# Issue order in an attention block: urgent exponentials and bank-emptying instructions, a later broadcast of 1/l, and outer sums laid elsewhere

## The chip, the cores and the metric

One core of one Trainium2 chip. Times are device microseconds of one execution; medians are given with the number of runs, and kernels are compared by the ratio of their mean times in the same rounds on the same chip (said again with the result). All quoted runs were in the fast state; the 41 runs of the kernel before that stand beside e1 lie within 0.31% (3239.23 to 3249.20 us). That matters here, because most differences are around 1%.

## The reference, cut to what matters

A block over 16 images of 512 channels and 32 x 32 pixels, all in float32:

```python
xn = group_norm(x, 8 groups)                       # per image
q, k, v = split(qkv_w @ xn + qkv_b)                # 512 -> 3 x 512
attn = softmax(q^T k / sqrt(128)) per head         # 4 heads, 1024 x 1024
out = x + proj_w @ (v attn^T) + proj_b
```

## The kernel before: the parts that the argument touches

The four heads of an image run one after the other. A head has 8 steps; in a step TensorE makes the transposed scores of 128 keys against 1024 queries in two halves, ScalarE takes their exponentials, and one step later TensorE adds v times those exponentials into a PSUM tile (PSUM is the memory that takes TensorE's results in this kernel; one 128 x 512 tile of it is called a bank here). TensorE's spare room in a head is filled with the big matrix products of a neighbouring image: q and k in heads 0 and 2, the projection in head 1, v in head 3. They are done by two levels of Strassen-like products, so VectorE makes sums of input blocks ("outer sums" t1 to t4 of the image, "inner sums" of their halves) and PSUM banks are emptied often, by copies on ScalarE and adds on VectorE.

The code is traced in program order and a scheduler then orders each engine's queue, by priority (which is the trace order, unless told otherwise) and by its own estimate of when things are ready. What stands ahead in a queue can cost time on the chip: in the trace of the kernel before, ScalarE was idle for 7.92 us before a copy that stood behind a transfer's issue (at 169.68 us, shown in the prediction).

The emptying of banks, which the change touches (cut):

```python
def kept_copy(n):                                   # in strassen(): x is a PSUM bank
    t[n] = upool.tile([P, HALF], F32, tag=n, ...)
    nc.scalar.copy(t[n][:, :width], t["x"][:, :width])

def out_(which, a, c=None):                         # in two_levels(): a is a PSUM bank
    ...
    if c is None:
        nc.scalar.copy(dst, view(a))
    else:
        nc.vector.tensor_add(dst, view(a), view(c))
```

The products of a group go by turns into a bank x and a bank y and mostly add to what is there already, so the product after next cannot start before the emptying is done (in the trace of the kernel before, v_y is held up so 30 times, for 13.7 us in sum and 0.7 at most). The broadcast of 1/l, the inverse of the softmax denominators, goes through DRAM: 1024 numbers are written as a row and read back onto all 128 partitions. Both transfers are issued on ScalarE's queue:

```python
def spread_inverse(b, h, step):
    if step == 0:
        row = rows_of[b, h] = dpool.tile([1, N], F32, ...)          # in DRAM
        nc.scalar.dma_start(row.rearrange(...), inverse.pop((b, h)))  # row <- r
        return
    rinv[b, h] = lpool.tile([P, N], F32, ...)
    nc.scalar.dma_start(rinv[b, h], rows_of.pop((b, h)).to_broadcast((P, N)))

for half in range(NH2):                             # in the loop over steps
    scores(s, half)                                 # matmul and exponential
    if j == 1 and s > NB:
        spread_inverse(*where(s - NB)[:2], half)
```

The second issue has to wait until the row has landed, which took 1.3 to 6.4 us from the row's issue in the trace of the kernel before (median 2.3, 63 rows). The image is normalised on ScalarE in steps 5 and 6 of head 1 of the image before, and its outer sums follow in steps 6 and 7.

## Time and profile before

| | before |
|---|---|
| median of the 3 runs at hand before the prediction | 3247.06 us (3245.63 to 3248.78) |
| span of the profiled execution | 3251.7 us |
| late starts of TensorE in it, in sum | 110.4 us |
| of these, before the first score | 12.4 us |
| tail | 2.3 us |

"Late starts" is the measure that the whole document uses. The records of two matmuls that follow each other without a hitch begin 0.429 us apart after a 512-wide one and 0.216 us after a 256-wide one (medians in the trace of the kernel before). Counted from a slightly lower line, 0.427 and 0.213 us, which the author set just below the smallest such intervals of that trace (0.428 and 0.215), whatever an interval has above it is a gap, and all gaps over 50 ns are summed. The page's own idle times are smaller, because a matmul's end is modelled and lies up to 0.17 us into the gap (a 512-wide record lasts 0.594 us in the mean, the next begins after 0.429). The lines of the page and of the waits are shown in the prediction below. In all such lines PE is TensorE, PEld its weight loads, DVE VectorE, ACT ScalarE, POOL GpSimd and SP SyncE; a q (ACTq) marks the issue of a transfer. A line in order of time has its start, its length (us), engine, source line, operation and `output<-inputs`; in brackets stands the idle time before it and what ended that.

### The profile page before, as it was taken

What the parts mean: (1) busy time and instruction counts of PE and PEld (TensorE: products, weight loads), DVE (VectorE), ACT (ScalarE), POOL (GpSimd) and SP (SyncE); (2) the same over time, 40 slices, a digit from 0 to 9 for tenths busy, and PEclk for the clock granted to TensorE, in tenths of its full rate; (3) what the DMA queues carried; (4) which work ended last, traced back from release to release, by engine and by line L of the source; (5) the groups of instructions that cost most, each with busy time, mean ns of one, the idle gap of its engine ahead of it and who ended that gap; (6) DMA issues with size and microseconds to landing.
All of it is one profiled execution on the core that took longest, in us unless ns stands there. A gap on an engine that the chain in (4) does not pass through costs nothing.

```text
span 3251.7 us, 34056 instructions
## 1 busy us (share of the span) xinstructions
PE 3185.4 (98%) x10474; PEld 2178.0 (67%) x10474; DVE 2633.3 (81%) x4625; ACT 1439.8 (44%) x2709; POOL 516.3 (16%) x922
## 2 busy tenths in 40 slices
PE   8999999999999999999999999999999999999999
PEld 6566666766666766667666666666666666666664
DVE  8868878788787888878788787987879878788784
ACT  2534435354353543535435354353534535344442
POOL 0011121111211112111121111212012120121100
PEclk9999999999999999999999999999999999999999
DMA  5555553545545455454554545545455453555531
GB/s 161 186 192 164 180 172 123 186 153 182 172 142 181 145 194 161 161 161 146 187 162 162 169 132 193 164 165 167 136 180 171 164 173 134 182 160 172 181 124 40
DMA packets 209388, 526.92 MB, mean 162 GB/s; under 512 B 32816, under 2 KB 65840, under 8 KB 209200
## 3 DMA queue, kind: packets, MB, share of 16 engines
q1 hardware_dynamic: 128992, 276.88, 27.5%
q0 software_dynamic: 66240, 212.39, 19.5%
q10 hardware_dynamic: 13968, 35.41, 3.4%
q8 instruction: 86, 1.41, 0.2%
q14 instruction: 102, 0.84, 0.1%
HBM read 389.56 MB, written 135.00 MB: 161 GB/s over the span
## 4 chain that ended last, share of the span: by engine, by line
PE 47%; issue 27%; DVE 16%; DMA 7%; POOL 2%; ACT 1%; ACTq 0%; POOLq 0%; SPq 0%; DVEq 0%
PE po L867 13%; PE s L772 13%; PE qk_x L548 6%; PE qk_y L548 5%; PE pp_x L548 4%; DVE qk_t L518 3%; PE pp_y L548 3%; DMA vd<-vu 2%; DVE xt L277 2%; DMA out_y<-y 2%; DMA y<-in_x 2%; DMA v<-vd 1%; DVE qk_r L567 1%; DVE vu L703 1%; DVE tot L785 1%
## 5 line engine op out<-in xcount | busy, mean ns | idle before, releaser
L772 PE MATMUL s<-qk,qk 128*128 128x512 f32 x2048 | 1049.0, 594 | 4.5 <-ACT p L777 4.3
L867 PE MATMUL po<-p,v 128*128 128x512 f32 x2048 | 1053.2, 596 | 0.0
L777 ACT ACTIVATE p<-s 128x512 f32<-128x512 f32 x1024 | 610.0, 596 | 895.9 <-PE s L772 817.1
L867 PEld LDWEIGHTS po<-p,v 128*128 128x128 f32 x2048 | 602.0, 303 | 319.1 <-issue 202.3
L785 DVE TENSOR_TENSOR tot<-tot,p 128x1024 f32<-128x1024 f32 x385 | 470.4, 1222 | 147.9 <-ACT p L777 146.2
L772 PEld LDWEIGHTS s<-qk,qk 128*128 128x128 f32 x2048 | 387.0, 190 | 114.1 <-issue 43.5
L548 PE MATMUL qk_x<-qk_t,w 128*128 128x256 f32 x1344 | 356.8, 384 | 9.4 <-DVE qk_t L518 3.5
L548 PEld LDWEIGHTS qk_x<-qk_t,w 128*128 128x128 f32 x1344 | 250.2, 190 | 170.0 <-issue 66.2
L448 ACT COPY qk_u<-qk_x 128x512 f32<-128x512 f32 (+1 forms) x256 | 136.1, 532 | 262.2 <-PE qk_x L548 208.3
L711 POOL DMA_DIRECT2D vd<-vu x120 | 66.3, 552 | 992.4 <-DVE vu L703 990.7
L567 DVE TENSOR_TENSOR qk_r<-qk_y,qk_u 128x512 f32<-128x512 f32 (+1 forms) x256 | 158.3, 619 | 40.1 <-ACT qk_u L448 26.3
L548 PE MATMUL pp_x<-pp_t,w_proj 128*128 128x256 f32 x630 | 170.8, 388 | 6.7 <-ACT pp_p L448 6.7
L567 DVE TENSOR_TENSOR v_r<-v_y,v_u 128x512 f32<-128x512 f32 (+1 forms) x120 | 76.5, 638 | 112.2 <-ACT v_u L448 82.0
L548 PE MATMUL v_x<-v_t,w_v 128*128 128x256 f32 x630 | 166.7, 381 | 0.0
L522 POOL DMA_DIRECT2D kept_t<-qk_t x240 | 129.2, 540 | 233.4 <-DVE qk_t L518 188.7
L756 POOL DMA_DIRECT2D out_y<-y x120 | 66.2, 552 | 627.4 <-DVE y L755 595.2
L548 PEld LDWEIGHTS pp_x<-pp_t,w_proj 128*128 128x128 f32 x630 | 114.0, 190 | 76.4 <-issue 22.5
L548 PEld LDWEIGHTS v_x<-v_t,w_v 128*128 128x128 f32 x630 | 118.6, 190 | 55.2 <-issue 19.1
L716 POOL DMA_DIRECT2D v<-vd x240 | 140.0, 590 | 83.8 <-issue 60.0
L548 PE MATMUL qk_y<-x,w 128*128 128x256 f32 x512 | 143.5, 382 | 0.0
L448 ACT COPY v_u<-v_x 128x512 f32<-128x512 f32 (+1 forms) x124 | 66.2, 534 | 164.8 <-PE v_x L548 125.0
L646 DVE SCALAR_TENSOR_TENSOR qk<-qk_r,qkb_sb,qk_r 128x512 f32<-128x512 f32 x192 | 137.3, 743 | 1.6
(204 smaller groups left out, 4486.0 us busy)
## 6 DMA issues: line engine op xcount, KB each, us to landing
w<-kept SPq DMA_DIRECT2D x90, 512.0 KB, 4.1
kept_t<-qk_t POOLq DMA_DIRECT2D x180, 256.0 KB, 4.4
v_t<-kept_t SPq DMA_DIRECT2D x180, 256.0 KB, 3.0
w<-kept SPq DMA_DIRECT2D x90, 384.0 KB, 3.9
rinv<-row ACTq DMA_DIRECT2D x63, 512.0 KB, 5.4
x<-in_x POOLq DMA_DIRECT2D x60, 512.0 KB, 5.0
vd<-vu POOLq DMA_DIRECT2D x120, 256.0 KB, 3.4
v<-vd POOLq DMA_DIRECT2D x240, 128.0 KB, 4.6
```

The lines of the kernel that those rows point to most:

```text
L448: nc.scalar.copy(t[n][:, :width], t["x"][:, :width])
L518: nc.vector.tensor_sub(to[:, i, :], inner_block(g, i, a), inner_block(g, i, c))
L522: nc.gpsimd.dma_start(t, to)
L548: nc.tensor.matmul(acc[:, ts(i, Q)], have["w"][t][:, i, slot, :], inner(i, bn), start=(first and i == 0), stop=True, skip_group_check=True,)
L567: nc.vector.tensor_add(dst, view(a), view(c))
L646: nc.vector.scalar_tensor_tensor(st[b, h][:, ts(half, HALF)], a, qkb_sb[:, i : i + 1], c, ALU.add, ALU.add)
L711: nc.gpsimd.dma_start(rows[which][ts(h, P), :], u)
L716: nc.gpsimd.dma_start(vs[b, pair][ts(q, BLK), half].rearrange("m h (k i) j -> m (h k) (i j)", k=n), rows[which].rearrange("(k m) (q e) -> ...
L772: nc.tensor.matmul(sc, ks[b, h][:, ts(j, P)], qs[b, h][:, ts(half, HALF)], start=True, stop=True)
L777: nc.scalar.activation(ps[s][:, ts(half, HALF)], sc, AF.Exp, scale=SCALE)
L785: added[b, h, j] = nc.vector.tensor_add(tot[b, h][:, i], tot[b, h][:, i], ps[s][:, i])
L867: nc.tensor.matmul(po[b, h][:, i], v_block(b, h, j), ps[s][:, i], start=(j == 0), stop=(j == NB - 1),)
```

## The change

Its intent: what TensorE waits for directly (exponentials, and copies and adds that empty PSUM banks) is put ahead of other work in the scheduler's choice; the broadcast is issued a step later, when its row has mostly landed; the image's outer sums are traced close to the step that reads them. No instruction is added or removed. `high_priority(40)` ranks an instruction as if it had been traced 40 instructions earlier. `issue_after(i)` keeps instructions behind `i` in its engine's queue; this part is called the pin below.

```diff
+URGENT = 40
...
-            nc.scalar.copy(t[n][:, :width], t["x"][:, :width])
+            with tc.high_priority(URGENT):
+                nc.scalar.copy(t[n][:, :width], t["x"][:, :width])
...
-                if c is None:
-                    nc.scalar.copy(dst, view(a))
-                else:
-                    nc.vector.tensor_add(dst, view(a), view(c))
+                with tc.high_priority(URGENT):
+                    if c is None:
+                        nc.scalar.copy(dst, view(a))
+                    else:
+                        nc.vector.tensor_add(dst, view(a), view(c))
...
-        nc.scalar.activation(ps[s][:, ts(half, HALF)], sc, AF.Exp, scale=SCALE)
+        with tc.high_priority(URGENT):
+            exps[s] = nc.scalar.activation(ps[s][:, ts(half, HALF)], sc, AF.Exp, scale=SCALE)
...
-                    plan[6 + r].append(lambda r=r: x_sums(b + 1, (r + 1,)))
+                plan[6].append(lambda: x_sums(b + 1, (1,)))
...
         elif h == 2:
             spread(plan, staggered(qk_groups(b + 1, 0)), 0, NB)
+
+            plan[0].insert(2, lambda: x_sums(b + 1, (2,)))
+            plan[1].append(lambda: x_sums(b + 1, (3,)))
...
-                if j == 1 and s > NB:
-                    spread_inverse(*where(s - NB)[:2], half)
+                if j in (1, 2) and half == 1 and s > NB:
+                    with tc.issue_after(exps[s].ins):
+                        spread_inverse(*where(s - NB)[:2], j - 1)
```

(Row 1 of the outer sums is t1, row 2 is now t2 alone, and the new row 3 is t3 and t4. Callers of the sums of o are adapted so that they do the same as before.)

More of the change, by code (lines that the diff above doesn't have):

```diff
@@ L271, in halves, with sums_of_b @@
         return b
-    def sums_of_b(b, rows=(1, 2), chunks=range(KC)):
+    def sums_of_b(b, rows=(1, 2, 3), chunks=range(KC)):
         def sub(o, i, j):
@@ L282, in sums_of_b, with x_sums @@
             sub("t2", "b22", "t1")
+        if 3 in rows:
             sub("t3", "t2", "b11")
             sub("t4", "b21", "t2")
-    def x_sums(b, rows=(1, 2)):
+    def x_sums(b, rows=(1, 2, 3)):
         if 1 in rows:
@@ L761, in fast_path @@
     ps, tot, po, rinv, last_eviction = {}, {}, {}, {}, {}
-    inverse, rows_of, added = {}, {}, {}
+    inverse, rows_of, added, exps = {}, {}, {}, {}
     steps = B * HEADS * NB
@@ L971, in last_projection @@
         l, recip = last_division(b, HEADS - 1)
-        sums_of_b(bl, (2,), (1,))
+        sums_of_b(bl, (2, 3), (1,))
         for r in range(2):
@@ L1046, in plan_head @@
                 plan[3].append(lambda: sums_of_b(ob[b], (1,)))
-                plan[5].append(lambda: sums_of_b(ob[b], (2,), (0,)))
+                plan[5].append(lambda: sums_of_b(ob[b], (2, 3), (0,)))
         elif h == 2:
             spread(plan, staggered(qk_groups(b + 1, 0)), 0, NB)
+            plan[0].insert(2, lambda: x_sums(b + 1, (2,)))
+            plan[1].append(lambda: x_sums(b + 1, (3,)))
         else:
```

## The prediction

> **What bounds the kernel now.** I read the page's busy shares first, then the order of time on TensorE, then the waits, and last the order of time around the longest gaps.
>
> ```profile
> PE 3185.4 (98%) x10474; PEld 2178.0 (67%) x10474; DVE 2633.3 (81%) x4625; ACT 1439.8 (44%) x2709; POOL 516.3 (16%) x922
> ```
>
> TensorE's matmul row is busy for 98% of the span of 3251.7 us; nothing else is near. But the ends of matmul records are modelled, so I measure TensorE by starts. TensorE in order of time, in a stretch where nothing holds it up:
>
> ```profile
> 999.87 1.02 PE L772 MATMUL s<-qk,qk 128*128 128x512 f32 x2
> 1000.73 1.02 PE L867 MATMUL po<-p,v 128*128 128x512 f32 x2
> 1001.59 0.60 PE L548 MATMUL qk_x<-qk_t,w 128*128 128x256 f32 x2
> 1002.02 1.02 PE L772 MATMUL s<-qk,qk 128*128 128x512 f32 x2
> ```
>
> A pair of 512-wide records takes 0.86 us from start to start (1000.73 - 999.87), so 0.43 each; a 256-wide one 0.215 (0.43 / 2). The trace holds 4155 of the first kind (2048 scores, 2048 weighted sums, some of the last projection) and 6188 of the second: 4155 x 0.428 + 6188 x 0.2155 = 1778 + 1334 = about 3112 us. The change removes no matmul, so this stays. The rest of the span, 3252 - 3112 = 140 us, is all there is to win. About 110 us of it are intervals between matmul starts that are over 50 ns too long: counted in the trace, 511 of them, 12.4 us before the first score at 69.8 us, 95.6 us in the main part, 2.3 us in the tail. The other 30 us are TensorE's idle beginning (its first matmul starts at 10.6 us) and the end (stores, the test of the flag), which the change doesn't touch.
>
> Who ends those gaps, from the view of waits (time in total, times, longest):
>
> ```profile
> ACT qk_p L448 <- DMA row<-r: 54.6, 12, 7.9
> PE v_y L548 <- DVE v_r L567: 13.7, 30, 0.7
> PE qk_y L548 <- DVE qk_t L518: 8.5, 14, 1.3
> PE pp_x L548 <- ACT pp_p L448: 6.7, 14, 1.5
> PE s L772 <- ACT p L777: 4.3, 6, 2.3
> PE qk_x L548 <- ACT qk_p L448: 3.5, 1, 3.5
> ```
>
> The reader is to see counts of 14 and 30: the same few places in each of the images (14 with an image before and after them; twice in 15). The lengths here are too small, since a modelled matmul end covers up to 0.17 us of each gap; by starts, the v_y gaps are 0.62 us in the mean, not 0.46.
>
> One such place for each cause, in order of time. VectorE, head 3 of image 5, a gap before v_y:
>
> ```profile
> 1239.63 1.25 DVE L877 TENSOR_TENSOR o<-o,rinv 128x1024 f32<-128x1024 f32 x1
> 1240.76 0.72 DVE L567 TENSOR_TENSOR v_r<-v_y,v_u 128x512 f32<-128x512 f32 x1
> 1241.54 1.13 PE L548 MATMUL v_y<-xt,w_v 128*128 128x256 f32 x4 [0.35 <-DVE v_r L567]
> ```
>
> The bank is emptied by v_r, whose other input was ready at 1238.7 (a copy begun at 1238.11 that takes 0.58), yet the division of 1.25 us was queued first. ScalarE, head 1 of the same image: a batch of normalisations stands before an exponential and a copy:
>
> ```profile
> 1143.92 2.93 ACT L82 ACTIVATE x<-x,sh,sc 128x512 f32<-128x512 f32 x4 [1.64 <-DVE sh L75]
> 1146.76 0.57 ACT L777 ACTIVATE p<-s 128x512 f32<-128x512 f32 x1
> 1147.24 0.35 ACT L448 COPY pp_p<-pp_x 128x256 f32<-128x256 f32 x1
> 1147.64 0.70 PE L548 MATMUL pp_x<-pp_t,w_proj 128*128 128x256 f32 x2 [0.38 <-ACT pp_p L448]
> ```
>
> And ScalarE's queue in image 0, with the broadcast of 1/l:
>
> ```profile
> 162.83 0.32 ACTq L816 DMA_DIRECT2D row<-r  x1
> 169.32 0.33 ACTq L821 DMA_DIRECT2D rinv<-row  x1
> 169.68 0.58 ACT L448 COPY qk_p<-qk_x 128x512 f32<-128x512 f32 x1 [7.92 <-DMA row<-r]
> 170.16 1.09 ACT L777 ACTIVATE p<-s 128x512 f32<-128x512 f32 x2
> ```
>
> From 162.8 to 169.3 the queue waits for the row to land before it can issue the load that reads it, and a copy and two exponentials stand behind.
>
> [...]98% busy, yet 110 us of late starts. [...]the copy behind the blocked issue lost 7.92 us. So order in the queue, which the change edits, decides. [...]The trace has 0.69 us for x's outer sums and 1.22 for tot: every non-urgent VectorE instruction costs an urgent one up to 1.2 us[...]. [...]Here row<-r lands after 1.3 to 6.4 us, median 2.3.
>
> **The change part by part.** No instruction is added or removed; all is order. Gaps below are sums over all images, by starts[...].
>
> 1. Urgent emptying of banks (copies and the adds or copies into R). The two v_y places in head 3 hold 12.6 + 9.3 = 21.9 us over 15 images. Taking the add at the next free slot saves a division of 1.13 us at one and a transpose of 1.1 at the other; both exceed the gap. I count 80%: -18 us. The pp_x place behind normalisations, 10.6 us over 14 images (0.65 plus 0.11 for the second matmul): one normalisation of 0.8 at most now stands before the copy, which was ready over 1 us earlier: -10.5.
> 2. Urgent exponentials. Image 0's gap of 2.4 us at 151.2 (2.92 us of normalisations before the exponential) goes: -2.4. In image 15 a bias that waits 3.5 us for a load stands before copies (1.8 us of gaps): -1.
> 3. The broadcast one step later (a step is about 6.2 us: 49.5 us of a head / 8), after that step's exponential. The row has landed by then in the median. The 54.6 us of ScalarE's idle time were mostly slack; what reached TensorE is 5.2 us at head 0's scores (11 to 13 images) and 5.3 in image 0: -4 and -4.
> 4. Outer sums of the image. Six subtractions of 0.69 (0.6 pipelined) stood ahead of head 2's inner sums. The four of t3 and t4 now come a step later, which takes 4 x 0.6 = 2.4 us out of the front. The gaps there (qk_y 13.3, qk_x 6.2, together 19.5 us over 14 images, 1.4 each) are shorter than 2.4. But t2 now falls behind the denominators (1.24 + 1.21 + about 1.3 of small ones = 3.7 us), and group 1's first product needs t2; it came late already in three images (3.7 us). I count half of 19.5: -10.
> 5. Small gaps of about 0.1 us (a weight load released late): some 25 us in all, mostly left: -2.
>
> Sum: -18 - 10.5 - 2.4 - 1 - 4 - 4 - 10 - 2 = -52 us. Against it, what is pushed back: inner sums qk_t and pp_t are not urgent yet TensorE needs them, and each urgent add can delay them by 0.7 us. I allow 1 us an image, 16 us. Net -36: 3247 - 36 = 3211 us.
>
> **The rivals.** (a) The wait only moves. VectorE is 81% busy, and in heads 1 to 2 it runs without a pause from 1143.8 to 1155.4; what urgent adds gain, inner sums, t2 and normalisation lose. For it: t2 behind the denominators could cost up to 2.5 us an image, 35 us, about all of the gain: 3240 to 3250. Against it: the v_y places are followed by work with slack. (b) Nearly every gap goes, as ScalarE is only 44% busy: 75 us less, 3172. Against: the 0.1 us gaps and the weight loads behind semaphores, and the start, have other causes. (c) The scheduler orders by its own estimates, so a new order can put a blocked DMA in front of ScalarE elsewhere; two us an image would make it 3240.
>
> **Range and chances.** 2% is 65 us, 59% of all late starts, and more than my gross sum: faster 0.05. Slower by 2% would need 4 us of new gaps in every image: 0.01. Within 2%: 0.94. Range 3188 to 3240.
>
> **What would show it.** Step 1: the v_y <- v_r and pp_x <- pp_p waits shrink from 13.7 and 6.7 us to under 4 together. Step 3: ScalarE's idle on row<-r falls from 54.6 to under 15. Step 4: the qk_y <- qk_t wait halves; if qk_x <- xt grows over 10 us, rival (a) has it. Busy times of all engines stay within 1%. I am wrong if late starts stay near 110 us in sum, or fall under 45.

## The result, and the profile after

| | before | after |
|---|---|---|
| median time, 4 runs each | 3247.92 us (3245.63 to 3251.33) | 3214.26 us (3210.56 to 3216.90) |
| ratio of the fast runs | | 0.9895, 95% interval 0.9878 to 0.9912 |
| span of the profiled execution | 3251.7 us | 3208.4 us |
| late starts in it | 110.4 us | 67.5 us |

A ratio here is the mean time of one kernel's fast runs over that of the other's fast runs of the same rounds, so it isn't quite the ratio of the medians. The difference of the medians is 33.7 us; the predicted one was 36. The profiled execution of before is a slow one of its kind and that of after the fastest, so their difference, 43.3 us, is larger.

TensorE does the same work, and its record shrinks only by gaps. The engines' line of the page of the changed kernel:

```profile
PE 3166.4 (99%) x10474; PEld 2181.6 (68%) x10474; DVE 2630.8 (82%) x4625; ACT 1442.0 (45%) x2709; POOL 528.8 (16%) x922
```

Late starts account for the whole difference: 3251.7 - 110.4 = 3141.3 us before, 3208.4 - 67.5 = 3140.9 after. This remainder is between 3140 and 3142 us in every profile of this study, whatever the kernel. So each experiment below can be read from its gaps alone.

Where they went, by place (sums over all images):

| place | before, us | after, us |
|---|---|---|
| head 3: v_y behind an add into v_r | 21.9 | 1.6 |
| start of head 2: products of the next image's q and k | 28.8 | 14.0 |
| end of head 1: pp_x behind a copy | 13.4 | 9.5 |
| start of head 1: pp_x | 0 | 4.7 |
| head 0, step 2: scores behind an exponential | 5.2 | 0 |
| image 0, head 2 | 8.1 | 5.7 |
| image 15, head 0 | 2.0 | 1.0 |
| before the first score | 12.4 | 10.2 |
| all the rest (many of about 0.1 us) | 18.6 | 20.8 |

The view of waits of the changed kernel (time in all, times, longest):

```profile
PE qk_y L553 <- DVE qk_t L523: 6.2, 6, 2.0
PE pp_x L553 <- ACT pp_u L453: 5.7, 14, 0.4
...
ACT v_r L571 <- DMA row<-r: 4.7, 4, 1.2
...
PE qk_x L553 <- DMA w<-kept: 2.8, 1, 2.8
...
ACT qk_r L571 <- DMA row<-r: 2.4, 2, 1.2
```

The 30 waits of v_y for v_r are no longer in the list, ScalarE's idle time behind the row fell from 57.2 us (54.6 of it before qk_p) to 4.7 + 2.4, and two waits of TensorE are there that were not before: pp_x now waits for pp_u where it waited for pp_p, and qk_x once for a load of weights. In order of time, the first place of the prediction (image 5, head 3) now reads

```profile
1224.96 0.72 DVE L573 TENSOR_TENSOR v_r<-v_y,v_u 128x512 f32<-128x512 f32 x1
1225.57 1.25 DVE L884 TENSOR_TENSOR o<-o,rinv 128x1024 f32<-128x1024 f32 x1
1225.93 1.03 PE L553 MATMUL v_y<-xt,w_v 128*128 128x256 f32 x4
```

The add stands ahead of the division, and v_y starts 0.87 us after the weighted sum before it, with no gap. At the end of head 1 the gap has moved by one product instead:

```profile
1137.32 0.81 ACT L85 ACTIVATE x<-x,sh,sc 128x512 f32<-128x512 f32 x1
1138.02 0.36 ACT L453 COPY pp_u<-pp_x 128x256 f32<-128x256 f32 x1
1138.44 0.70 PE L553 MATMUL pp_x<-pp_t,w_proj 128*128 128x256 f32 x2 [0.40 <-ACT pp_u L453]
```

The product before it began at 1136.58 and was through at about 1137.2; a normalisation took ScalarE at 1137.32, and the urgent copy came after its 0.8 us. Urgent here means next in the queue as the scheduler saw it, not an interruption.

In image 0 the wait for the row gave its place to another, a load of weights:

```profile
162.28 0.33 ACTq L828 DMA_DIRECT2D rinv<-row  x1
...
166.15 1.74 PE L553 MATMUL qk_x<-x,w 128*128 128x256 f32 x4 [2.83 <-DMA w<-kept]
```

And the gap costs more than its own length. Two stretches around it (length; busy time and number of instructions of PE, PEld, DVE, ACT and POOL; granted TensorE clock; share of the DMA engines; GB/s):

```profile
163.00:166.00 3.00, 0.32 (x1) 0.00 (x0) 3.00 (x5) 1.09 (x2) 0.53 (x1) 1.00 0.95 316
166.00:170.00 4.00, 3.85 (x10) 3.14 (x11) 0.54 (x2) 0.59 (x1) 0.00 (x0) 0.57 1.01 373
```

TensorE stood still in nearly all of the first stretch, and in the next its granted clock is 0.57 (0.5 from 166.47 to 169.88 us in the clock record): seven 256-wide products after the gap start 0.43 us apart in place of 0.22. The kernel before had the same after its gap of 3.7 us there (clock 0.5 from 170.81 to 174.22 us). This will matter in the experiments.

### The profile page after: what moved, and what is told of

The parts are those of the page before. It is cut to its first block, busy times and chain, and to the rows that moved or that the text cites. A ratio compares the mean times of both kernels' runs of the same rounds, so it can differ in the third digit from the quotient of the medians.

```text
span 3208.4 us, 34028 instructions
## 1 busy us (share of the span) xinstructions
PE 3166.4 (99%) x10474; PEld 2181.6 (68%) x10474; DVE 2630.8 (82%) x4625; ACT 1442.0 (45%) x2709; POOL 528.8 (16%) x922
## 4 chain that ended last, share of the span: by engine, by line
PE 72%; DVE 19%; issue 4%; DMA 4%; POOL 1%; ACT 0%; SPq 0%; ACTq 0%; POOLq 0%; DVEq 0%
PE po L874 19%; PE s L778 19%; PE qk_x L553 9%; PE qk_y L553 7%; PE v_x L553 6%; PE v_y L553 4%; PE pp_x L553 4%; PE pp_y L553 2%; DVE tot L792 2%; DVE qk L652 2%; DVE qk_r L573 2%; DMA y<-in_x 2%; DVE qk_r L620 2%; DVE qk_t L523 1%; DVE y L761 1%
```

## The experiments

Twelve kernels ran, each timed in five rounds against the kernel before. All gave correct results. The theory that the prediction stands for (theory A below) is that the three parts add up, urgency being the larger half. In the table, "banks" are the copies and adds that empty banks, "exps" the exponentials. The rivals are told with each run. For each, the table has the ratio, the gaps per image by head (mean over images 1 to 14) and all gaps of the profiled execution.

| run | urgent | pin | outer sums | ratio (95% interval) | head 0 | head 1 | head 2 | head 3 | all gaps, us |
|---|---|---|---|---|---|---|---|---|---|
| before | - | - | - | 1 | 0.46 | 1.43 | 2.13 | 1.54 | 110.4 |
| e1 | all | - | - | 1.0110 (1.0094 to 1.0125) | 4.87 | 1.47 | 1.17 | 0.18 | 135.9 |
| e2 | - | yes | - | 0.9996 (0.9987 to 1.0004) | 0.09 | 1.42 | 1.77 | 1.54 | 97.6 |
| e3 | - | - | yes | 0.9993 (0.9984 to 1.0001) | 0.30 | 1.43 | 1.71 | 1.53 | 96.7 |
| e4 | - | yes | yes | 0.9986 (0.9980 to 0.9993) | 0.09 | 1.42 | 1.87 | 1.54 | 97.7 |
| e5 | all | yes | - | 0.9915 (0.9902 to 0.9929) | 0.10 | 1.47 | 1.37 | 0.18 | 74.5 |
| e6 | all | - | yes | 1.0114 (1.0099 to 1.0130) | 4.84 | 1.47 | 1.32 | 0.20 | 138.2 |
| e7 | banks | yes | yes | 0.9889 (0.9874 to 0.9905) | 0.12 | 1.39 | 0.70 | 0.18 | 62.8 |
| e8 | exps | yes | yes | 0.9991 (0.9983 to 0.9999) | 0.09 | 1.23 | 2.32 | 1.54 | 102.2 |
| the change | all | yes | yes | 0.9895 (0.9878 to 0.9912) | 0.09 | 1.46 | 1.09 | 0.19 | 67.5 |
| e9 | all | other queue | yes | 0.9884 (0.9869 to 0.9899) | 0.09 | 1.47 | 1.32 | 0.20 | 66.5 |
| e10 | banks, inner sums | yes | yes | 0.9914 (0.9900 to 0.9927) | 0.09 | 0.95 | 0.42 | 1.47 | 74.4 |
| e11 | as e10, one chunk on VectorE | yes | yes | 0.9917 (0.9904 to 0.9931) | 0.09 | 0.86 | 0.67 | 1.48 | 74.1 |
| e12 | banks | other queue | yes | 0.9876 (0.9860 to 0.9893) | 0.18 | 1.37 | 0.81 | 0.19 | 62.3 |

**e1, urgency alone.** The kernel before with the three `high_priority` blocks of the diff above and nothing else.

> The kernel before with the urgency of exponentials, copies and bank-emptying adds alone (no pin, outer sums as before). Theory A, urgency is the larger half: the v_y <- v_r gaps of head 3 (21.9 us by starts) go, those of head 2 (29 us) stay, head 0's scores behind the row (5.2 us) stay or halve: 22 us less, ratio about 0.993. Rival B, the three parts are one effect (urgent work does harm until the sums are out of its way): under 8 us less, ratio over 0.9975.

It is slower by 1.1%: 3278.86 us in the median of 4 runs against 3245.16. Neither theory had that. Head 3's gaps fell as foretold, from 1.54 to 0.18 us an image (-19 us in 14 images), and head 2's by 1 us, but head 0's rose by 4.4 us. The waits of this run:

```profile
PE qk_x L552 <- ACT qk_u L452: 45.2, 17, 3.8
```

One of them in order of time (image 5, head 0):

```profile
1066.03 0.32 ACTq L822 DMA_DIRECT2D row<-r  x1
...
1070.04 0.33 ACTq L827 DMA_DIRECT2D rinv<-row  x1
1070.41 0.59 ACT L452 COPY qk_u<-qk_x 128x512 f32<-128x512 f32 x1 [3.36 <-DMA row<-r]
...
1071.05 1.22 PE L552 MATMUL qk_x<-qk_t,w 128*128 128x256 f32 x2 [2.90 <-ACT qk_u L452]
```

The same place of the kernel before:

```profile
1064.38 0.32 ACTq L816 DMA_DIRECT2D row<-r  x1
...
1065.30 0.58 ACT L448 COPY qk_u<-qk_x 128x512 f32<-128x512 f32 x1
1069.96 0.33 ACTq L821 DMA_DIRECT2D rinv<-row  x1
```

In both, ScalarE's queue stops at the broadcast until the row has landed; from the row's issue to the broadcast's it is 4.0 us in e1 and 5.6 before. Before, the copy that TensorE needs stood ahead of the broadcast; what stood behind the stop, the next copy and an exponential, had nearly enough slack (TensorE was 0.30 us late here). With urgency the order came out the other way round, so the copy, urgent or not, waited behind the broadcast and TensorE with it. With the pin, in the changed kernel, the copy stands first again, and the broadcast comes when the row has landed:

```profile
1051.04 0.59 ACT L453 COPY qk_u<-qk_x 128x512 f32<-128x512 f32 x1 [1.12 <-PE qk_x L553]
...
1052.82 0.33 ACTq L823 DMA_DIRECT2D row<-r  x1
...
1058.87 0.33 ACTq L828 DMA_DIRECT2D rinv<-row  x1
```

In e1 a second cost follows. Two stretches from there on (columns as above):

```profile
1070.00:1077.00 7.00, 5.95 (x10) 3.44 (x11) 2.61 (x4) 2.76 (x5) 2.90 (x5) 0.51 1.00 280
1077.00:1081.00 4.00, 4.00 (x16) 3.00 (x16) 2.31 (x3) 0.60 (x1) 1.08 (x2) 1.00 0.63 189
```

TensorE works at about half speed until 1077 (granted clock 0.51 in the first stretch, 1.00 in the second). So it went after 11 of the 14 gaps of this kind (2.1 to 4.0 us), in nine of them for 3.4 us and in two, as here, for 6.8. Over the run the mean granted clock is 0.993 where the kernel before has 0.999, and 16 us of the gaps lie in step 2 of head 0, where for the most part TensorE waits for nothing and is only slower (0.43 us late after each 512-wide record in that image).

**e2, the pin alone.** The kernel before with the last part of the diff (`issue_after`, `j in (1, 2)`).

> The kernel before with the pinned broadcast of 1/l alone. Theory A: only the gap at head 0's scores (5.2 us) goes, ratio 0.998 to 0.999, and ScalarE's idle time on row<-r falls from 54.6 us to under 10. Rival C, a blocked ScalarE queue is behind most late emptyings: 20 us less or more, ratio 0.994, and the v_y <- v_r waits fall too.

Ratio 0.9996: not distinguishable from 1. In the profile head 0's gaps went from 0.46 to 0.09 us an image, the 5 us foretold, and ScalarE's idle time on the row from 57.2 to 12.3 (under 10 was expected); the v_y waits stayed at 13.6 us. So nearly all of what the stop costs ScalarE was slack in the kernel before, and the rival, that it makes most emptyings late, is out.

**e3, the outer sums alone**, and **e4, pin and outer sums without urgency.** Edits: the parts of the diff with `x_sums` and `sums_of_b`; in e4 also the pin.

> The kernel before with the outer sums of the image laid later, alone. Theory A: the gaps at the start of head 2 (29 us by starts) halve, nothing else changes: 12 to 15 us less, ratio 0.9955. Rival: t2 behind the denominators makes group 1's first product late, the wait moves from qk_y <- qk_t to qk_x <- xt and the time stays, ratio 0.999 to 1.001.

> The changed kernel with nothing urgent: pin and outer sums alone. Theory A, the parts add: the sum of the two single runs before, about 18 us less, ratio 0.9945, and the v_y <- v_r waits of 13.7 us stay whole. Rival B, urgency is needed for the others to pay: ratio over 0.998.

Ratios 0.9993 and 0.9986; the sum of e2 and e3 would be 0.9989. These two do add, but to 4 or 5 us, not to 18. In e3 the qk_y gaps at the start of head 2 were 12.4 us, those of qk_x 6.2, against 13.3 and 6.2 before. VectorE in image 5 of e3, at the start of head 2:

```profile
1153.26 1.24 DVE L795 STREAM_TRANSPOSE tt<-tot 128x1024 f32<-128x1024 f32 x1
1154.42 0.38 DVE L519 TENSOR_TENSOR qk_t<-x 128x256 f32<-128x256 f32 x1
1154.72 1.21 DVE L797 TENSOR_REDUCE part<-tt 128x32 f32<-128x1024 f32 x1
```

The outer sums are gone from here (t2 begins at 1159.16), but the inner sums qk_t that TensorE waits for still alternate with the two long instructions of the denominators, as they did before. My expectation of half those gaps failed; the rival had the time right, though not the place. The wait did not move to the products that read t2; on the contrary, what went is a wait of qk_x for xt, an outer sum, of 3.7 us in three images.

**e5 and e6, the change without the outer sums and without the pin.** e5 is e1 plus the pin; e6 is e1 plus the outer sums.

> The changed kernel with the outer sums as before: urgency and pin. Theory P (urgency gains 22 us at the banks, but alone it puts copies that TensorE waits for behind the blocked broadcast; the pin takes that away, and the outer sums are a minor third): ratio 0.990 to 0.9935, the v_y <- v_r and the qk_x <- qk_u waits both gone. Rival S (the outer sums are needed too): ratio 0.997 or more.

> The changed kernel with the broadcast of 1/l as before: urgency and outer sums. Theory P: as slow as urgency alone, ratio 1.005 to 1.012, with waits of qk_x <- qk_u of 40 us or so in head 0 behind row<-r. Rival S: the outer sums cure it, ratio under 0.997.

Ratios 0.9915 and 1.0114. Theory P holds: without the pin everything else is 1.1% slower than before, and with it 1% faster. e6 has the same waits of qk_x for qk_u as e1 (46.5 us, 17 times). The pin is worth 0.0219 x 3247 = 71 us beside urgency and 0.0004 x 3245 = 1 us alone. Leaving the outer sums out costs 0.9915 - 0.9895 = 0.002, some 6 us, with intervals that overlap.

**e7 and e8, which of the urgent instructions.** In e7 the exponentials are not urgent; in e8 only they are:

```diff
-        with tc.high_priority(URGENT):                      # e7
-            exps[s] = nc.scalar.activation(...)
+        exps[s] = nc.scalar.activation(...)
```

> The changed kernel with the exponentials at their normal place; copies and bank-emptying adds stay urgent. Theory P: the v_y gaps are ended by the adds alone, so nearly the whole gain stays: ratio 0.989 to 0.992; image 0's gap at its scores (2.4 us before) may come back. Rival E (exponentials, which release both the scores' banks and the weighted sums, carry the gain): ratio over 0.995.

> The changed kernel with only the exponentials urgent; copies and bank-emptying adds at their normal place. Theory P: the v_y gaps of 22 us return: ratio 0.996 to 0.999. Rival E: ratio 0.989 to 0.992.

0.9889 and 0.9991: the copies and adds that empty banks carry all of the gain, the exponentials none. In e8 head 3's gaps are back at 1.54 us an image. In e7 the gap of 2.4 us at image 0's scores came back, as expected, and head 2's gaps fell from 1.09 to 0.70; against the whole change 0.9889 is not a proven improvement.

**e9, the broadcast on another queue.** This takes away the suspected cause in another way than the pin. It is e6 with both transfers issued by SyncE:

```diff
-            nc.scalar.dma_start(row.rearrange(...), inverse.pop((b, h)))
+            nc.sync.dma_start(row.rearrange(...), inverse.pop((b, h)))
...
-        nc.scalar.dma_start(rinv[b, h], rows_of.pop((b, h)).to_broadcast((P, N)))
+        nc.sync.dma_start(rinv[b, h], rows_of.pop((b, h)).to_broadcast((P, N)))
```

> Urgency and outer sums without the pin (the slow version, 1.0114), but both transfers of 1/l issued from SyncE's queue instead of ScalarE's. Theory P (the harm is copies standing in ScalarE's in-order queue behind an issue that waits for the row): the qk_x <- qk_u waits of 46.5 us go and the time is near the changed kernel's, ratio 0.989 to 0.995. Rival T (the transfer's early start is the harm, as a load beside others): ratio stays over 1.003. Third possibility: SyncE's weight loads behind the blocked issue come late, waits on w <- kept appear, ratio between.

From 1.0114 to 0.9884, without a pin. The transfers are the same and still have to wait for the row; it is SyncE's queue that waits now (total, times, longest):

```profile
SPq L828 <- DMA row<-r: 93.8, 51, 5.0
```

94 us of waiting there do not show in TensorE's waits: there is none for a load of weights in this run. So the harm in e1 and e6 is the standing behind a blocked issue in the queue of an engine that computes (3.36 us of ScalarE's time at the place shown in e1), and this is shown twice, by the pin and by the queue.

**e10 and e11, the gaps that are left.** e10 is e7 with the inner sums urgent too (`with tc.high_priority(URGENT)` around the subtraction in `make_sum`); e11 also normalises the last of four chunks on VectorE.

> Exponentials not urgent (the fastest so far, 0.9889), and VectorE's inner sums urgent too. If the gaps left at the start of head 2 (qk_x and qk_y behind inner sums, 8.6 us by starts) are a matter of order alone: they go, 6 to 9 us less, ratio 0.986 to 0.987. Rival: urgent inner sums push the bank-emptying adds back, ratio 0.989 to 0.992.

> As the run with urgent inner sums, and the last of four chunks of the image normalised on VectorE, to shorten what stands before the copies at the end of head 1 (8.3 us of gaps there). If ScalarE's normalisations are what makes these late: 5 to 8 us less than the run before, ratio 0.984 to 0.986. Rival: VectorE, 82% busy, is the one that is late there: no change or worse, ratio 0.987 to 0.992.

0.9914 and 0.9917, which is 0.0025 and 0.0028 above e7. The intervals overlap by a little (e10 from 0.9900, e7 to 0.9905), so the times alone leave it just open; the gaps, 74.4 us against 62.8, go the same way. In e10 head 2's gaps went from 0.70 to 0.42 us an image and head 1's from 1.39 to 0.95, but head 3's came back, from 0.18 to 1.47:

```profile
PE v_y L554 <- DVE v_r L574: 16.6, 15, 1.1
```

VectorE at one of these places (image 5):

```profile
1240.58 1.26 DVE L792 TENSOR_TENSOR tot<-tot,p 128x1024 f32<-128x1024 f32 x1
1241.74 0.43 DVE L574 TENSOR_TENSOR v_r<-v_y,v_u 128x256 f32<-128x256 f32 x1
```

The rival was right as to the place. With the inner sums urgent, the emptying add is no longer ahead: an accumulation of 1.26 us stands before it, and TensorE idles 1.1 us. In e11 the freed 1.6 us of ScalarE changed head 1 by 0.09 us and nothing in the time.

**e12, the two best together.** Urgent banks, outer sums, transfers on SyncE's queue, no pin.

> The two versions that did best put together: copies and bank-emptying adds urgent, exponentials not, outer sums laid later, both transfers of 1/l on SyncE's queue and no pin. If the two gains (0.0006 against the changed kernel by the normal exponentials, 0.0011 by the queue) add: ratio 0.986 to 0.988. Rival: both take away the same gaps or are noise, ratio 0.988 to 0.990. Either way the v_y and qk_x <- qk_u waits stay away.

0.9876, in the range where the two gains add: 3205.0 us (3201.04 to 3209.28, 4 runs). It beats the kernel before for certain and has the lowest median of all; its interval overlaps those of the changed kernel, e7 and e9, so its lead over these is not settled.

## Why the prediction was right, and which steps of it were not

The time, 3211 predicted against 3214.26, and the bound (all is in TensorE's late starts, at most 110 us of them, no engine's busy time changes) were right. The sum behind it was right in part by luck: pp_x and image 0 gave 10.6 us less than was counted on, and what is pushed back came 11.3 us smaller than was set against it.

- **The bound.** Right: 42.9 us of late starts went, and the span less its late starts is the same in all profiles to 1 us. Busy times stayed within 1% except GpSimd's, 516.3 to 528.8 us (2.4% more).
- **Step 1, v_y.** Predicted -18, measured -20.3 (21.9 to 1.6). e5 to e8 show that urgency of the bank-emptying instructions does it.
- **Step 1, pp_x behind the normalisations.** Predicted -10.5, measured -3.9: 13.4 us at the end of head 1 became 9.5. The step that failed is "one normalisation of 0.8 at most now stands before the copy, which was ready over 1 us earlier": that held for pp_p, but the normalisations, spread out, now stand before pp_u, which is not ready early. The wait was moved by one product, not removed.
- **Step 2, exponentials.** The gap at image 0's scores went as told (2.4 to 0.8 us). As a part of the change it is worth nothing that can be measured (e7).
- **Step 3, the broadcast.** -4 at head 0's scores was right (5.2 to 0; e2). The -4 in image 0 was not: that gap shrank from 5.7 to 4.9 us because a load of weights took the row's place. What was wrong is the frame: counted as a separate gain of 8 us, it is in truth the condition for step 1, worth 71 us beside it (e5, e6, e9). The rival (c) named this danger, a new order that puts a blocked DMA in front of ScalarE, at two us an image. It is 4.4, and it came up in the kernel without the pin. The waits of before could have warned me: they show a queue that stops for up to 7.9 us, and the change reorders what stands around it.
- **Step 4, outer sums.** Predicted -10 of the 19.5 us before qk_y and qk_x. These fell by 5.5, to 14.0; the whole start of head 2 fell by 14.8, but mostly through urgency: head 2's gaps are 1.17 us an image with urgency alone, 1.71 with the outer sums alone, 1.09 with all. Their own share is some 6 us (e5), within the noise.
- **What is pushed back**, +16. Of this kind are the 4.7 us at the start of head 1: in image 5 a weight load of pp_x waits there, by its semaphore, for an inner sum pp_t that ends at 1095.79 and is queued behind the urgent add of 1094.26. Right in kind, over three times too large; the waits for the inner sums of head 2 fell in sum.
- **Rival (a)**, t2 behind the denominators: qk_x never waited for it after the change; the denominators delay the inner sums instead.
- **What would show it.** v_y <- v_r and pp_x <- pp_p fell to none, as told, but pp_x <- pp_u (5.7 us) stands for the latter. ScalarE's idle on the row fell to 7.1 us, under 15. The qk_y wait fell from 8.5 to 6.2, not by half. Late starts ended at 67.5, between the 45 and 110 given.

Left open: which of the urgent instructions turn the order round, the exponentials, the copies or the adds, as e7 and e8 kept the pin, and whether the adds alone carry the gain without the copies; why the scheduler, given urgency, puts the broadcast ahead of those copies (its estimates are not in a trace; that it treats the row as landed sooner than it does would fit, but was not tested), and what decides in which images qk_y at the start of head 2 waits (in the changed kernel 8 of 14 images have a gap there, three of them of 1.7 to 2.2 us).

## What to carry to other kernels

Before giving instructions a higher priority, look for issues in the same engine's queue that wait for a transfer: here what ended up behind them waited too, urgent or not (an urgent copy behind 3.36 us of idle ScalarE in e1), and a change that helps by 1% hurt by 1% here until such issues were moved to a queue that computes nothing, or later. Make urgent only what the bound engine waits for directly; urgency is relative, and a further class (here the inner sums, e10) can take it from the first. Parts of a scheduling change need not add, so run each alone and each left out.

## What the traces show of the row and the clock

- Moving two transfers of a head from ScalarE's to SyncE's queue changed the time from 1.0114 to 0.9884 of the kernel before (e6, e9), as no copy stood behind an issue that waited for the row any more: the waits of qk_x for qk_u fell from 46.5 us (17 times) to 3.4 (3 times).
- The row of 4 KB, which ScalarE issues beside other traffic, landed after 1.3 to 6.4 us (median 2.3) in the kernel before.
- A stretch at half clock came after gaps that were shorter than itself. In all 14 traces the clock record changes in steps of 3.41 us. Cut each trace, from 80 to 3150 us, into stretches of that length in step with its changes, and count TensorE as busy from each matmul's start for its 0.43 or 0.21 us: the 41 stretches at full clock before a fall were busy for 0 to 39%, the 12,505 others for 36% or more. A gap of 2.43 us in e7 was followed by 3.4 us at half clock, one of 2.44 at the same place of the kernel before was not; there it lay from 148.60 to 151.04 us, across the step at 150.33, and the stretch before that step was busy for 56%. That the place of a gap within the steps decides is the author's reading of these counts; it was not tested by itself.
